# Layer 2 of a four-layer graph network: one block-diagonal projection in banks of its own, and the pair's preparation on other units

## The chip, the cores and the metric

The kernel runs on one core of a Trainium2 chip. The metric is the device time of one launch in microseconds, the median of several runs. The profile is of one further execution. Its abbreviations: PE is TensorE's matmul, PEld its weight load, DVE is VectorE, ACT ScalarE, POOL GpSimd, SP SyncE.

## What is computed

Four graph layers follow each other on x of shape 16 x 1024 x 64 with one 1024 x 1024 adjacency matrix; after each comes a residual and a layer normalization. The change is in layer 2 (and touches code that layer 0 shares):

```python
def _L2_gnn_ref(input, adj, W, a):
    h = jnp.matmul(input, W)
    s1 = jnp.einsum('bnf,f->bn', h, a1)
    s2 = jnp.einsum('bnf,f->bn', h, a2)
    e = s1[:, :, None] + s2[:, None, :]
    e = jnp.where(e > 0, e, ALPHA * e)
    masked = jnp.where(adj[None, :, :] > 0, e, NEG_INF)
    attention = jax.nn.softmax(masked, axis=-1)
    h_prime = jnp.matmul(attention, h)
    return jax.nn.elu(h_prime)
...
x = _layernorm(x + _L0_gnn_ref(x, L0_gnn_W, L0_gnn_a, adj), axis=-1)
x = _layernorm(x + _L1_gnn_ref(x, ...), axis=-1)
x = _layernorm(x + _L2_gnn_ref(x, adj, L2_gnn_W, L2_gnn_a), axis=-1)
x = _layernorm(x + _L3_gnn_ref(x, adj, ...), axis=-1)
```

## The kernel before

Layers 0 and 2 are made by one function, `gat_layer`. A batch b has 1024 nodes, which lie as C = 8 chunks of P = 128; D = 64 features; HALF = 512, CH = 4. The attention weight of node m for node n is rewritten as a product in which the softmax's row factor cancels, so that a unit k (128 of the nodes summed over) is one DVE instruction, `e` = max(G, q) times the transposed adjacency (L959, 128 x 1024), and one `product` on PE: two matmuls (L971) with 64 value columns as weights, one for each half of 512 nodes. Their outputs lie on partitions 0 to 63 and 64 to 127 of one accumulator bank `y`. In layer 2 (`zero_mean`) the 64th value column holds p alone, since a feature whose mean is zero follows from the other 63, and this row of `y` is the softmax's sum.

After eight units a batch goes through its tail: `evict` copies `y` to SBUF (ACT, L989); `project` multiplies it by the weights on PE; `divide` takes the sums out of PSUM, inverts them and scales (DVE, L1014, L1016, two of L1019), then exponentiates for the elu (`m`, ACT, L1026); `residual` is two DVE operations (L1031, L1032); `norm` eight `bn_stats` (L1040), and for the second batch of a pair a chain of small operations for the moments; `root`, `shift` and `store` finish it (ACT, DVE, ACT: eight activations `x`, L775).

`project` in layer 2 has twelve matmuls: four with the two columns of `ind`, which pick the sums (L1001), and eight of 64 columns with `w_out` (128 x 64, the weights twice), each from one half of the partitions (L1005). They go into two tiles `po` of the pool `ps_t` (two banks, shared with the transposes and scores below).

The preparation is made for a pair of batches (b even, b + 1): `prep_x` transposes x in two halves (`pxT`, PE L898, copied by ACT, L899); `prep_s` has eight matmuls of 4 columns for the node scores (`ps`, L904); `prep_top` copies these on DVE (L912), takes a maximum, and reduces it over the partitions on POOL (`gtop`, L916); `prep_p` (`down`, `up` on DVE, p and q on ACT); `prep_G` in two halves, each two matmuls (`pg`, L939) and an exponential of ACT (L940); `prep_v` scales the values on ACT for one batch (eight of L946 and a copy).

Layer 2 is recorded under a manual schedule: the order in which the Python code issues instructions is the order on PE, ACT, DVE and POOL. The main loop goes over t (the batch) and k (the unit). In each step it issues `unit` (DVE) for k, then the `product` of two units earlier (LAG = 2), then the tasks that the dictionary `slots` holds for (t, k). A task of batch b is placed with `at(b + t, k, task)`. The tail of a batch stands at (1, 1), (1, 3), (1, 4), (1, 6), (1, 7), (2, 0), (2, 2) and `store` at (3, 6) or (3, 2), that is while the next batches' units run. So "unit 3" below is a place k = 3 in the step of some batch t; in an even t the transposes, scores and top of the next pair are placed, in an odd t p and G. Layer 0 isn't under the manual schedule.

[...] In layer 2 the pools `ps_t` (2), `ps_a` (2, for `y`) and `ps_g` (2) take six. Layer 3 starts behind layer 2 with other pools; its `project` has the form that the change brings to layer 2, with `wb` as the weights (L1276, L1280, L1286).

Of the kernel before, what the change touches and what calls it, by code (L numbers as in the profile page):

```python
# [8 lines left out]
F32 = mybir.dt.float32  # L9
# [4 lines left out]
ALU = mybir.AluOpType  # L14
AX = mybir.AxisListType

P = 128
# [561 lines left out]
def fast_path(  # L579
# [24 lines left out]
    nc = tc.nc  # L604
    B, N, D = x.shape
    C = N // P
# [5 lines left out]
    HALF = N // 2  # L612
    CH = C // 2

    const = ctx.enter_context(tc.tile_pool(name="const", bufs=1))
# [71 lines left out]
    def bc_last(ap, n):  # L687

        return ap.unsqueeze(2).to_broadcast([P, ap.shape[1], n])
# [150 lines left out]
    def gat_setup(w, name, zero_mean):  # L840
        wd, w1, w4, ind, a_sb = (w[k] for k in ("wd", "w1", "w4", "ind", "a"))
        wT = const.tile([D, P], F32, tag=f"{name}_wT", name=f"{name}_wT")
        transposed(wT, wd, P, D)
        pa = ps_t.tile([P, HALF], F32, tag="t", name=f"{name}_pa")
        nc.tensor.matmul(pa[:, :2], wT, a_sb, start=True, stop=True)
        wa = const.tile([P, 2], F32, tag=f"{name}_wa", name=f"{name}_wa")
        nc.vector.tensor_copy(wa, pa[:, :2])
        nc.vector.tensor_scalar(w1, ones, wa[:, 0:1], None, ALU.mult)
        nc.vector.memset(w4, 0.0)
        nc.vector.memset(ind, 0.0)  # L850
        for i in range(2):
            rows = slice(i * D, (i + 1) * D)
            nc.vector.tensor_copy(w4[rows, i : i + 1], wa[rows, 0:1])
            nc.vector.tensor_copy(w4[rows, 2 + i : 3 + i], wa[rows, 1:2])
        if zero_mean:


            less = const.tile([P, P], F32, tag=f"{name}_less", name=f"{name}_less")
            nc.vector.tensor_copy(less, ident)
            for i in range(2):  # L860
                rows = slice(i * D, (i + 1) * D)
                end = (i + 1) * D - 1
                nc.vector.tensor_scalar(
                    less[rows, rows], ident[rows, rows], ident[rows, end : end + 1], None, ALU.subtract
                )
                nc.vector.tensor_copy(ind[rows, i : i + 1], ident[rows, end : end + 1])
            pw = ps_t.tile([P, HALF], F32, tag="t", name=f"{name}_pw")
            nc.tensor.matmul(pw[:, :D], less, wd, start=True, stop=True)
            w_out = const.tile([P, D], F32, tag=f"{name}_wo", name=f"{name}_wo")
            nc.vector.tensor_copy(w_out, pw[:, :D])  # L870
        else:
            w_out = wd

            for r in range(4):
                rows = slice(r * 32, (r + 1) * 32)
                nc.vector.tensor_copy(ind[rows, r % 2 : r % 2 + 1], ident[rows, r * 32 : r * 32 + 1])
        w["out"] = w_out

    def gat_layer(w, name, zero_mean, extra, first, own, ordered):
# [7 lines left out]
        xT, G, pq, vals, only, stats = {}, {}, {}, {}, {}, {}  # L887
# [10 lines left out]
                nc.tensor.transpose(pt[:, j, :], x_pair(b, h * CH + j), ident)  # L898
            nc.scalar.copy(xT[b][:, h * HALF : (h + 1) * HALF], pt.rearrange("p j q -> p (j q)"))  # L899

        def prep_s(b):
            pt = ps_t.tile([P, HALF], F32, tag="t", name="ps12")
            for c in range(C):
                nc.tensor.matmul(  # L904
                    pt[:, 4 * c : 4 * c + 4], xT[b][:, c * P : (c + 1) * P], w4, start=True, stop=True
                )
            pq[b] = pt

        def prep_top(b):
            pt = pq[b]  # L910
            s = s12[:, b // 2]
            nc.vector.tensor_copy(s, pt[:, : 4 * C].rearrange("p (c f) -> p c f", f=4))  # L912
            top = small.tile([P, 1], F32, tag="top", name="top")
            nc.vector.tensor_reduce(top, s[:, :, 2:4], AX.XY, ALU.max)
            gtop = small.tile([P, 1], F32, tag="gtop", name="gtop")
            nc.gpsimd.partition_all_reduce(gtop, top, P, bass_isa.ReduceOp.max)  # L916
            pq[b] = gtop

        def prep_p(b):
            gtop = pq[b]  # L920
            down = small.tile([P, 1], F32, tag="down", name="down")
            nc.vector.tensor_scalar(down, gtop, -1.0, None, ALU.mult)
            up = small.tile([P, 1], F32, tag="up", name="up")
            nc.vector.tensor_scalar(up, gtop, 1.0 - ALPHA, None, ALU.mult)
            s2 = s12[:, b // 2, :, 2:4]
            p = small.tile([P, C, 2], F32, tag="p", name="p")
            nc.scalar.activation(p, s2, AF.Exp, bias=down)
            q = small.tile([P, C, 2], F32, tag="q", name="q")
            nc.scalar.activation(q, s2, AF.Exp, bias=up, scale=ALPHA - 1.0)
            pq[b] = (p, q, up)  # L930
# [23 lines left out]
        def attention(b):  # L954
# [40 lines left out]

            def project():
                y, t = held["s"]
                pos = [ps_t.tile([P, HALF], F32, tag="t", name="po") for _ in range(2)]
                tot = pos[0][:, CH * D : CH * D + 2 * CH].rearrange("p (j h) -> p j h", h=2)
                for j in range(CH):  # L1000
                    nc.tensor.matmul(tot[:, j, :], t[:, j * P : (j + 1) * P], ind, start=True, stop=True)  # L1001
                for j in range(CH):
                    for h, po in enumerate(pos):
                        rows = slice(h * D, (h + 1) * D)
                        nc.tensor.matmul(  # L1005
                            po[:, j * D : (j + 1) * D], y[rows, j * P : (j + 1) * P], w_out[rows, :],
                            start=True, stop=True,
                        )
                held["p"] = pos, tot

            def divide():
                pos, tot = held["p"]
                total = sums[:, b, :]
                nc.vector.tensor_scalar(total.rearrange("p (h j) -> p j h", h=2), tot, 1e-30, None, ALU.max)  # L1014
                rt = small.tile([P, C], F32, tag="rt", name="rt")
                nc.vector.reciprocal(rt, total)  # L1016
                held["v"] = ep.tile([P, C, D], F32, tag="v", name="v")
                for h, po in enumerate(pos):
                    nc.vector.tensor_tensor(  # L1019
                        held["v"][:, h * CH : (h + 1) * CH, :],  # L1020
                        po[:, : CH * D].rearrange("p (j d) -> p j d", d=D),
                        bc_last(rt[:, h * CH : (h + 1) * CH], D), ALU.mult,
                    )

                held["m"] = ep.tile([P, C, D], F32, tag="m", name="m", bufs=4)
                nc.scalar.activation(held["m"], held["v"], AF.Exp)  # L1026

# [36 lines left out]
            slots.setdefault((t, k), []).append(task)  # L1064

        work = [attention(b) for b in range(B)]
        for b in range(B):
            end = (3, 6) if b % 2 == 0 else (3, 2)
            for task, (t, k) in zip(work[b][2], ((1, 1), (1, 3), (1, 4), (1, 6), (1, 7), (2, 0), (2, 2), end)):
                at(b + t, k, task)  # L1070
        ahead = []
        for b in range(0, B, 2):
            chain = [(lambda b=b, h=h: prep_x(b, h), -2, h) for h in range(2)]
            chain += [(lambda b=b: prep_s(b), -2, 2), (lambda b=b: prep_top(b), -2, 3)]
            chain += [(lambda b=b: prep_p(b), -1, 1)]
            chain += [(lambda b=b, h=h: prep_G(b, h), -1, 2 + h) for h in range(2)]
            chain += [(lambda b=b: prep_v(b), -1, 4), (lambda b=b: prep_v(b + 1), 0, 4)]
            for task, t, k in chain:
                if b + t < 0:
                    ahead.append(task)  # L1080
                else:
                    at(b + t, k, task)
# [127 lines left out]
    def prep_v(b):  # L1210
        v = l3a.tile([P, C, D], F32, tag="vals", name=f"vals_{b}")
        nc.scalar.copy(v[:, :, : D - 1], xb(b)[:, :, : D - 1])
        nc.vector.memset(v[:, :, D - 1 : D], 1.0)
        vals[b] = v
# [421 lines left out]
                at(b + t, p, task, where)  # L1636

    with tc.tile_pool(name="ps_g", bufs=1, space=bass.MemoryType.PSUM, reuse_waits="tile") as ps_g, tc.tile_pool(
        name="gat2", bufs=2, reuse_waits="tile"
    ) as gp:  # L1640
        places = [(15, j) for j in (0, 1, 2, 3, 4, 5, 6, 7)]
        extra = {p: [task] for p, task in zip(places, ahead)}
        for p, task in zip(((0, 0), (0, 1), (0, 3), (0, 7), (1, 3), (1, 7)), last):
            extra.setdefault(p, []).append(task)

        def first(ahead):
            for task in ahead:
                task()

        ending = gat_layer(later["w2"], "l2", True, extra, first, 5, True)  # L1650
# [128 lines left out]
```

## Time and profile before

| | us |
|---|---|
| median of 3 runs | 2162.24 (2161.66 to 2167.61) |
| the profiled execution | 2170.64 |
| its span, first to last instruction | 2168.8 |
| layer 0, first product to last projection | about 31 to 297 |
| layer 2, first `e` to the last projection's end | 467.7 to 728.3 |
| `e` of a unit, DVE, from one to the next | 1.20 |
| a product (two matmuls), PE, back to back at full and half clock | 0.86, 1.72 |
| `pxT`, four transposes | 0.65 |
| eight `bn_stats` | 1.03 |

The page counts time as busy when an instruction was on the engine; a matmul of fp32 shows as two records, so "x8" is four matmuls. In timeline lines the first number is the start, the second the time covered, and in square brackets stands the engine's idle time just before it with what ended it. The clock is the share of TensorE's full speed that was granted.

### The profile page before, as it was taken

The numbers are of one execution on the slowest core, as the hardware profiler recorded it, in microseconds if no ns is written. First come the engines' busy times: TensorE is split into PE (matmuls) and PEld (weight loads), VectorE is DVE, ScalarE is ACT, GpSimd is POOL, SyncE is SP. The second block draws the span as 40 slices with busy tenths as digits, with TensorE's granted clock in tenths as the row PEclk, the third lists the DMA queues.
The fourth block names the chain that finished last, engine by engine and source line by source line (L and its number), as shares of the span: only waits on it lengthen the run. The fifth ranks groups of instructions, "written<-read, shape, count | busy, mean of one in ns | idle before, by whom it ended". The sixth has DMA issues, their size and how long they took to land.

```text
span 2168.8 us, 26641 instructions
## 1 busy us (share of the span) xinstructions
PE 2047.2 (94%) x10321; PEld 866.2 (40%) x10321; DVE 1852.5 (85%) x3221; ACT 1227.5 (57%) x1965; POOL 51.0 (2%) x77
## 2 busy tenths in 40 slices
PE   7999979998898899999999999999999999999993
PEld 3333347753433333333333333333333433343331
DVE  5888889978988877798898898889889889888997
ACT  4454556555535666566655665655665665565541
POOL 0000000000000000000000000000000000000001
PEclk8999989988978999999999999999999999999997
DMA  6000000000000200000000000000000000000000
GB/s 162 1 1 1 1 1 1 1 1 1 1 1 1 72 6 1 1 1 6 1 6 5 1 6 1 6 5 1 6 6 1 6 1 6 6 1 6 1 7 15
DMA packets 23656, 18.92 MB, mean 9 GB/s; under 512 B 19361, under 2 KB 19426, under 8 KB 23522
## 3 DMA queue, kind: packets, MB, share of 16 engines
q1 hardware_dynamic: 23218, 17.11, 2.8%
q8 instruction: 83, 1.36, 0.3%
q14 instruction: 51, 0.42, 0.1%
q10 hardware_dynamic: 304, 0.03, 0.0%
HBM read 12.95 MB, written 4.19 MB: 8 GB/s over the span
## 4 chain that ended last, share of the span: by engine, by line
PE 73%; DVE 21%; ACT 4%; issue 1%; DMA 0%; POOL 0%; SPq 0%; POOLq 0%; DVEq 0%; ACTq 0%
PE y L1259 18%; PE s L1247 17%; PE y_l L971 8%; PE s L1344 5%; PE y L1371 4%; DVE e L1252 4%; PE u_l L982 3%; DVE e L959 3%; PE po L1276 3%; PE po L1531 3%; PE po L1005 2%; PE pg L939 2%; PE po L1001 1%; PE ps L904 1%; ACT e L1251 1%
## 5 line engine op out<-in xcount | busy, mean ns | idle before, releaser
L1251 ACT ACTIVATE e<-s,shift 128x1024 f32<-128x1024 f32 x512 | 542.9, 1111 | 243.2 <-PE s L1247 237.8
L1252 DVE TENSOR_TENSOR e<-e,aT 128x1024 f32<-128x1024 f32 x512 | 602.6, 1220 | 87.7 <-ACT e L1251 85.6
L1247 PE MATMUL s<-hT 64*128 64x512 f32 x2048 | 509.9, 612 | 15.5 <-DVE top L1188 8.6
L1259 PE MATMUL y<-e,vals 128*64 128x512 f32 x2048 | 490.6, 601 | 3.2 <-ACT yT L1266 1.3
L959 DVE SCALAR_TENSOR_TENSOR e<-G_l,q,aT 128x1024 f32<-128x1024 f32 x256 | 319.9, 1276 | 20.5 <-ACT G_l L940 12.4
L971 PE MATMUL y_l<-e,vals_l 128*64 128x512 f32 x1024 | 278.8, 660 | 27.9 <-DVE e L959 26.3
L1247 PEld LDWEIGHTS s<-hT 64*128 64x128 f32 x2048 | 182.5, 186 | 256.0 <-issue 170.8
L1259 PEld LDWEIGHTS y<-e,vals 128*64 128x64 f32 x2048 | 131.0, 136 | 330.6 <-issue 258.0
L1349 ACT ACTIVATE e<-s,shift 128x1024 f32<-128x1024 f32 x128 | 141.8, 1113 | 85.1 <-PE s L1344 74.9
L1351 DVE TENSOR_TENSOR me<-e,aT 128x1024 f32<-128x1024 f32 x128 | 155.8, 1220 | 16.8 <-ACT e L1349 16.5
L1362 DVE SCALAR_TENSOR_TENSOR junk<-e,aN 128x1024 bf16<-128x1024 f32 x128 | 155.9, 1218 | 0.2
L1371 PE MATMUL y<-me,h2v 128*64 128x512 f32 x512 | 135.3, 609 | 10.5 <-DVE me L1351 10.4
L1344 PE MATMUL s<-h2T 64*128 64x512 f32 x512 | 136.3, 610 | 4.6 <-DVE h2v L1331 4.4
L971 PEld LDWEIGHTS y_l<-e,vals_l 128*64 128x64 f32 x1024 | 65.3, 146 | 184.9 <-issue 75.4
L1531 PE MATMUL po<-hi,aR 128*128 128x512 f32 x256 | 101.9, 398 | 2.7 <-ACT hi L1516 1.1
L775 ACT ACTIVATE x<-m,bn_shift,bn_rstd 128x64 f32<-128x64 f32 x256 | 88.7, 432 | 23.2 <-DVE bn_shift L766 23.2
L1531 PE MATMUL po<-lo,aR 128*128 128x512 f32 x256 | 99.8, 391 | 0.0
L1306 ACT COPY zT<-pzT 128x1024 f32<-128x1024 f32 x32 | 32.4, 1012 | 78.3 <-PE pzT L1305 78.3
L1276 PEld LDWEIGHTS po<-wb,yT 128*128 128x128 f32 x512 | 62.0, 190 | 34.0 <-issue 21.1
L1276 PE MATMUL po<-wb,yT 128*128 128x130 f32 x512 | 73.8, 287 | 1.3 <-ACT e L1251 1.2
L982 PE MATMUL u_l<-e,only 128*32 128x512 f32 x512 | 72.0, 612 | 0.0
L1344 PEld LDWEIGHTS s<-h2T 64*128 64x128 f32 x512 | 46.6, 186 | 63.7 <-issue 41.4
(214 smaller groups left out, 2019.9 us busy)
## 6 DMA issues: line engine op xcount, KB each, us to landing
adj<-in_adj_dram SPq DMA_DIRECT2D x16, 512.0 KB, 4.4
x<-in_x_dram SPq DMA_DIRECT2D x16, 256.0 KB, 5.0
out_dram<-res SPq DMA_DIRECT2D x16, 256.0 KB, 2.0
wl<-in_L_gnn_Wh_dram SPq DMA_DIRECT2D x2, 64.0 KB, 5.3
wo<-in_L_gnn_Wo_dram SPq DMA_DIRECT2D x1, 64.0 KB, 5.0
l_wd<-in_L_gnn_W_dram ACTq DMA_DIRECT2D x2, 16.0 KB, 4.7
l_wd<-in_L_gnn_W_dram SPq DMA_DIRECT2D x2, 16.0 KB, 2.0
bo<-in_L_gnn_bo_dram SPq DMA_DIRECT2D x1, 32.0 KB, 3.3
```

The source lines that it names most:

```text
L959: nc.vector.scalar_tensor_tensor(e, G[b - b % 2][:, b % 2, :], pq[b - b % 2][1][:, k, b % 2 : b % 2 + 1], aT[:, k, :], ALU.max, ALU.mult,)
L971: nc.tensor.matmul(held["y"][h * D : (h + 1) * D, :], vals[b][:, k, :], e[:, h * HALF : (h + 1) * HALF], start=(k == 0), stop=(k == C - 1),)
L1247: nc.tensor.matmul(s[:, i, :], hT[rows, k * P : (k + 1) * P], hT[rows, cols], start=True, stop=True)
L1251: nc.scalar.activation(e, s, AF.Exp, bias=shifts[b, n])
L1252: nc.vector.tensor_tensor(e, e, bc_mid(aT[:, k, cols], 2), ALU.mult)
L1259: nc.tensor.matmul(held[h][i * D : (i + 1) * D, :], vals[b][:, k, :], e[:, i, :], start=(k == 0), stop=(k == C - 1),)
L1276: nc.tensor.matmul(o[:, j // 2, j % 2, :], held["y"][:, c * P : (c + 1) * P], wb[:, n, :], start=True, stop=True,)
L1344: nc.tensor.matmul(s[:, i, :], hT[rows, (i + k // CH) % 2, k % CH * P : (k % CH + 1) * P], hT[rows, 0, :], start=True, stop=True,)
L1351: nc.vector.tensor_tensor(m, e, aT[:, k, :].rearrange("p (i q) -> p i q", i=2), ALU.mult)
L1362: nc.vector.scalar_tensor_tensor(junk, held.pop(k).rearrange("p i q -> p (i q)"), 1.0, aN[:, k, :], ALU.mult, ALU.mult, accum_out=sums[:, ...
L1371: nc.tensor.matmul(held["o"][h * D : (h + 1) * D, :], vals["out", b][:, k, :], e[:, h, :], start=(k == 0), stop=(k == C - 1),)
L1531: nc.tensor.matmul(po.rearrange("p q k f -> p (q k f)"), aR[:, k, ic * P : (ic + 1) * P], e[:, k].rearrange("p q k f -> p (q k f)"), start ...
```

## The change

In `gat_setup`, for layer 2, `w_out` becomes 128 x 130: the weights as two diagonal blocks, zeros elsewhere, and the two columns of `ind` behind them. In `project` one matmul for each of four chunks then gives both halves and their sums; outputs go to a tile of two banks from a new pool `ps_p`, two chunks to a bank. `divide` reads this layout with four-dimensional views; layer 0 keeps its matmuls and gets the same views of its own layout. The preparation in layer 2 is placed anew, with `prep_s` cut in two halves of four chunks; layer 0 keeps its places.

```diff
-            w_out = const.tile([P, D], F32, tag=f"{name}_wo", name=f"{name}_wo")
-            nc.vector.tensor_copy(w_out, pw[:, :D])
+            w_out = const.tile([P, P + 2], F32, tag=f"{name}_wo", name=f"{name}_wo")
+            nc.vector.memset(w_out, 0.0)
+            for i in range(2):
+                rows = slice(i * D, (i + 1) * D)
+                nc.vector.tensor_copy(w_out[rows, i * D : (i + 1) * D], pw[rows, :D])
+            nc.vector.tensor_copy(w_out[:, P : P + 2], ind)
...
-        def prep_s(b):
-            pt = ps_t.tile([P, HALF], F32, tag="t", name="ps12")
-            for c in range(C):
+        def prep_s(b, chunks):
+            if chunks[0] == 0:
+                pq[b] = ps_t.tile([P, HALF], F32, tag="t", name="ps12")
+            for c in chunks:
                 nc.tensor.matmul(
...
             def project():
                 y, t = held["s"]
+                if zero_mean:
+                    pt = ps_p.tile([P, 2, HALF], F32, tag="p", name="po")
+                    o = pt[:, :, : 2 * (P + 2)].rearrange("p t (c f) -> p t c f", c=2)
+                    for j in range(CH):
+                        nc.tensor.matmul(
+                            o[:, j // 2, j % 2, :], y[:, j * P : (j + 1) * P], w_out, start=True, stop=True
+                        )
+                    held["p"] = [o[:, :, :, h * D : (h + 1) * D] for h in range(2)], o[:, :, :, P : P + 2]
+                    return
                 pos = [ps_t.tile([P, HALF], F32, tag="t", name="po") for _ in range(2)]
...
-                nc.vector.tensor_scalar(total.rearrange("p (h j) -> p j h", h=2), tot, 1e-30, None, ALU.max)
+                nc.vector.tensor_scalar(total.rearrange("p (h t c) -> p t c h", h=2, t=2), tot, 1e-30, None, ALU.max)
...
                     nc.vector.tensor_tensor(
-                        held["v"][:, h * CH : (h + 1) * CH, :],
-                        po[:, : CH * D].rearrange("p (j d) -> p j d", d=D),
-                        bc_last(rt[:, h * CH : (h + 1) * CH], D), ALU.mult,
+                        held["v"][:, h * CH : (h + 1) * CH, :].rearrange("p (t c) d -> p t c d", t=2), po,
+                        rt[:, h * CH : (h + 1) * CH].rearrange("p (t c) -> p t c", t=2).unsqueeze(3).to_broadcast(
+                            [P, 2, 2, D]
+                        ), ALU.mult,
                     )
...
             chain = [(lambda b=b, h=h: prep_x(b, h), -2, h) for h in range(2)]
-            chain += [(lambda b=b: prep_s(b), -2, 2), (lambda b=b: prep_top(b), -2, 3)]
-            chain += [(lambda b=b: prep_p(b), -1, 1)]
-            chain += [(lambda b=b, h=h: prep_G(b, h), -1, 2 + h) for h in range(2)]
-            chain += [(lambda b=b: prep_v(b), -1, 4), (lambda b=b: prep_v(b + 1), 0, 4)]
+            if zero_mean:
+                chain += [(lambda b=b, h=h: prep_s(b, range(h * CH, (h + 1) * CH)), -2, 5 + h) for h in range(2)]
+                places = (-2, 7), (-1, 1), (-1, 4), (-1, 6), (-1, 2)
+            else:
+                chain += [(lambda b=b: prep_s(b, range(C)), -2, 2)]
+                places = (-2, 3), (-1, 1), (-1, 2), (-1, 3), (-1, 4)
+            chain += [(task, *place) for task, place in zip((
+                lambda b=b: prep_top(b), lambda b=b: prep_p(b), lambda b=b: prep_G(b, 0),
+                lambda b=b: prep_G(b, 1), lambda b=b: prep_v(b),
+            ), places)]
+            chain += [(lambda b=b: prep_v(b + 1), 0, 4)]
...
     with tc.tile_pool(name="ps_g", bufs=1, space=bass.MemoryType.PSUM, reuse_waits="tile") as ps_g, tc.tile_pool(
+        name="ps_p", bufs=1, space=bass.MemoryType.PSUM, reuse_waits="tile"
+    ) as ps_p, tc.tile_pool(
         name="gat2", bufs=2, reuse_waits="tile"
     ) as gp:
```

More of the change, by code (lines that the diff above doesn't have):

```diff
@@ L899, in prep_x @@
             nc.scalar.copy(xT[b][:, h * HALF : (h + 1) * HALF], pt.rearrange("p j q -> p (j q)"))
-        def prep_s(b):
-            pt = ps_t.tile([P, HALF], F32, tag="t", name="ps12")
-            for c in range(C):
+        def prep_s(b, chunks):
+            if chunks[0] == 0:
+                pq[b] = ps_t.tile([P, HALF], F32, tag="t", name="ps12")
+            for c in chunks:
                 nc.tensor.matmul(
-                    pt[:, 4 * c : 4 * c + 4], xT[b][:, c * P : (c + 1) * P], w4, start=True, stop=True
+                    pq[b][:, 4 * c : 4 * c + 4], xT[b][:, c * P : (c + 1) * P], w4, start=True, stop=True
                 )
-            pq[b] = pt
         def prep_top(b):
@@ L1008, in project @@
                         )
-                held["p"] = pos, tot
+                held["p"] = (
+                    [po[:, : CH * D].rearrange("p (t c d) -> p t c d", t=2, d=D) for po in pos],
+                    tot.rearrange("p (t c) h -> p t c h", t=2),
+                )
             def divide():
@@ L1066, in gat_layer @@
         work = [attention(b) for b in range(B)]
+        ends = ((1, 1), (1, 3), (1, 4), (1, 6), (1, 7), (2, 0), (2, 2))
         for b in range(B):
             end = (3, 6) if b % 2 == 0 else (3, 2)
-            for task, (t, k) in zip(work[b][2], ((1, 1), (1, 3), (1, 4), (1, 6), (1, 7), (2, 0), (2, 2), end)):
+            for task, (t, k) in zip(work[b][2], (*ends, end)):
                 at(b + t, k, task)
```

## The prediction

> **What bounds the kernel now.** I read the page first, then busy times by stage, then who waited for whom on VectorE inside layer 2, then the timeline there. On the page:
>
> ```profile
> PE 2047.2 (94%) x10321; PEld 866.2 (40%) x10321; DVE 1852.5 (85%) x3221; ACT 1227.5 (57%) x1965; POOL 51.0 (2%) x77
> ...
> PE   7999979998898899999999999999999999999993
> ...
> PEclk8999989988978999999999999999999999999997
> ```
>
> PE (TensorE) looks like the bound everywhere, but PEclk dips in slices 9 to 13, which is layer 2 (about 467 to 728 us). The busy times of four stretches (layers 0, 1, 2, 3) show that layer 2 is different:
>
> ```profile
> 60.00:300.00 240.00, 236.64 (x1520) 87.27 (x1516) 202.18 (x450) 117.43 (x321) 3.06 (x6) 1.00 0.00 1
> 320.00:456.00 136.00, 132.54 (x646) 108.48 (x645) 130.82 (x297) 81.11 (x159) 0.00 (x0) 1.00 0.00 1
> 467.00:728.00 261.00, 230.56 (x1144) 101.77 (x1144) 220.60 (x464) 128.45 (x376) 9.34 (x9) 0.83 0.02 7
> 740.00:2100.00 1360.00, 1336.80 (x6501) 515.13 (x6500) 1180.22 (x1762) 826.55 (x978) 27.26 (x45) 1.00 0.02 5
> ```
>
> Columns: stretch, length, then busy us of PE, PEld, DVE, ACT, POOL, then the granted clock. Layers 0 and 3 keep PE 98% busy at clock 1.00. In layer 2 PE has 30 us of idle and a clock of 0.83, and DVE (VectorE) has 40 us of idle. For what DVE waited, in the list of waits between 470 and 735 us (total, times, longest):
>
> ```profile
> DVE l_sums L1014 <- PE po L1005: 29.5, 12, 4.0
> DVE v L1031 <- ACT m L1026: 2.5, 2, 1.7
> ...
> DVE l_s L912 <- PE ps L904: 1.7, 2, 1.2
> ```
>
> One wait dominates: `divide` on DVE waits for the last matmul of `project`. The timeline of one even batch shows why PE is late there:
>
> ```profile
> 563.64 1.95 PE L904 MATMUL ps<-l_w,xT_l 128*128 128x4 f32 x16
> ...
> 566.53 1.05 PE L1001 MATMUL po<-l_ind,yT_l 128*128 128x2 f32 x8
> ...
> 567.51 1.83 PE L1005 MATMUL po<-l_wo,yT_l 64*128 64x64 f32 x16
> ...
> 569.37 0.17 DVE L1014 TENSOR_SCALAR l_sums<-po 128x8 f32<-128x8 f32 x1 [1.80 <-PE po L1005]
> ```
>
> Within 5.6 us PE runs eight small matmuls for the scores (`prep_s`), one attention product, then twelve small ones for the projection. DVE stands 1.80 us. The counter-example is batch 14, which has no pair left to prepare:
>
> ```profile
> 696.63 1.05 PE L1001 MATMUL po<-l_ind,yT_l 128*128 128x2 f32 x8
> ...
> 697.61 1.11 PE L1005 MATMUL po<-l_wo,yT_l 64*128 64x64 f32 x16
> ...
> 699.07 0.17 DVE L1014 TENSOR_SCALAR l_sums<-po 128x8 f32<-128x8 f32 x1
> ```
>
> No idle stands in brackets: the same long projection without the preparation ahead of it is hidden behind DVE's units.
>
> DVE's floor: from `divide` at 487.88 to the one six pairs later at 686.05 are 198.2 us, 33.0 a pair, of which the idle entries of the timeline sum to 27.4 (25.3 at L1014, 1.7 at L1031, 0.4 at L912). So 28.5 us a pair is DVE's own work.
>
> [...] stretches of 2 us in layer 2 stand at 0.50 or 1.00 or on an edge between (566 to 568: 0.93, 568 to 570: 0.50), and the dips follow either idle (608 to 612, PE busy 1.76 of 4 us) or the run of small matmuls above. [...] (at 492.47 `m` came only after eight `x` of L775 queued ahead, and DVE stood 1.66 us for it). [...] The pools then hold 2+2+2+2 banks. [...]
>
> **The change part by part.**
>
> *Projection.* Twelve matmuls a batch go, four of 128x130 come. The old ones take 2.02 us on PE at full clock (696.63 to the next product at 698.65), 3.7 at half (631.43 to 635.14). Layer 3 has the new form already (L1276):
>
> ```profile
> 758.55 1.16 PE L1276 MATMUL po<-wb,yT 128*128 128x130 f32 x8
> 759.64 2.85 PE L1247 MATMUL s<-hT 64*128 64x512 f32 x12
> ```
>
> So 1.09 us, 0.93 less; at half clock it isn't shown, between 1.09 (if issue sets it) and 2.18; I take 1.9. The DVE part keeps its sizes: L1280 and L1286 of layer 3 read the same layout at 171 and 419 ns, L1014 and L1019 take 170 and 419, so 0. The bank pair of its own removes waits for `ps_t` buffers (at most what batch 15 shows, PE held before 711.42 by `hsq`); I take 0 to 0.5 us once, and 0 in the sum. In exchange layer 3's third score tile has to wait for batch 15's `divide` if it lies on these banks: v ends some 1.3 us after the projection, two tiles ahead of it take 1.7, so 0.
>
> *`prep_s` and `prep_top`.* The 1.88 us of eight score matmuls leave the place ahead of `project` (unit 2) for units 5 and 6, in two halves. Their new neighbours are the units where `divide` (1.12), `residual` (1.30) and `norm` (1.03, with moments 1.9) keep DVE away from making `e`, so PE has room there. `prep_top` moves past `norm` to unit 7; its POOL reduction (1.24) now has two units of 1.20 until `down` instead of six. Cover 2.4 against about 1.5, cost 0.
>
> *`prep_G`.* Two matmuls (0.95 each half, 2.0 cold) leave units 2 and 3 for 4 and 6, so the odd batches lose the first half ahead of `project`. What is queued on ACT matters: in the changed order it is `m`, G half 0, eight `x` of a stored batch, G half 1, and DVE's first unit of the next batch needs half 1. From the end of `v`: `m` 0.67, G 1.11, eight `x` 2.76, G 1.11, sum 5.7. DVE from there: two units 2.4, residual 1.3, a unit 1.2, `bn` 1.03, sum 5.9. It just fits; I charge 0.15 us a pair, 1 in all, and up to 1.4 a pair if PE is cold there.
>
> *`prep_v`* of an even batch goes to unit 2 (2.1 us of ACT), before `m` is wanted 2.4 us and more later: 0. No DMA moves, and SP's and POOL's order is unchanged.
>
> *Set-up*: a memset and three small copies on DVE in layer 0 (0.4 us), which PE bounds: 0.
>
> What remains of the wait: at full clock, from `e1`'s end PE needs a product (0.86 to 1.08) and 1.09, DVE three units (3.6): slack 1.4 us. Entirely at half clock, even batch, from `e7`'s end: products 3 x 1.72, transposes 1.1, projection 1.9, sum 8.2, against `bn` 1.03 and five units 6.0: 1.2 us late. In an odd batch DVE has moments 0.9, top 0.35 and shift 0.7 besides and PE no transposes, so nothing is late. Dips will not go away (at the end of even batches PE still waits for DVE), so I leave 0.4 us for each of seven even batches, 3 us.
>
> Sum on the profile: removed 27.4 (L1014 without the last batch), 1.7 (L912), 0.9 (the last projection, where PE sets the pace into layer 3), 30.0; left 3 and 1. Gain 26, so 2170.6 (span 2168.8 and 1.9 around it) becomes 2144.6. What is late next is DVE itself. The median of the runs is 2162.2, 8.4 below the profiled run. Either profiling added that everywhere (then 2136), or the profiled run had more dips in layer 2, the only long stage without a clock of 1.00 (then its extra wait is part of the 26, and 2144.6 stands). I can't tell which and take the middle, 2140.
>
> **The rivals.**
> (1) *PE goes on being late.* Spreading the small matmuls leaves PE with less work and as many gaps, and dips fall on every even batch: 7 x 1.2 of projection and 7 x 1.0 of late G, 15 of 30 remain. Time 2162.2 - 12 = 2150. For it: dips at 512, 612, 646 and 677 begin where DVE starves PE, and that stays. Against: PE recovers within 3 to 7 us, before unit 3 in most.
> (2) *Slower: the clock falls.* PE's work a pair at full clock is then 16 products x 0.86, 1.3, 1.9, 1.9 and 2 x 1.09, about 21 us. Against 28.5 of DVE it is busy 74% only; if the clock stays low for it, a pair takes 21/clock, and that passes the present 33.0 plus 0.9 (6.5 us over seven pairs) below a clock of 0.62. At 0.58 it is 36 us a pair, +22, 2184. Against: a cold PE is a full PE, and full stretches restored it every time here; no stretch of 40 us in layer 2 is below 0.76.
> (3) *The G chain.* If half 1 comes 1.5 us late in each pair, 10 us are given back: 2150.
> (4) *The waits were hidden anyway*: would need layer 3 to absorb them. It has PE 98% busy, so an earlier start is an earlier end: 2162.
>
> **How the numbers follow.** Forecast 0.72, (1) 0.14, (3) 0.07, (4) 0.03, (2) 0.04. The floor for the range: all 30 removed and the profile's 8.4 off, 2132. The top: rivals (1) and (3) with the unprofiled base uncertain, 2152. A difference of 0.3% (6.5 us) is what can be told from no change. Faster: the forecast, (1) and (3), 0.93; within 0.3%: (4), 0.03; slower: (2), 0.04.
>
> **What would show it.** Right: L1014's successor waits less than 5 us in all in layer 2, the pair period is 28.5 to 29.5, DVE over 95% busy between 480 and 700 us, the four wide matmuls take about 1.1 us, layer 3 keeps its length. Wrong: a clock below 0.75 in layer 2, DVE's `e` waiting for G by over 1 us a pair, `down` waiting for POOL, or `m` late for `residual`.

## The result, and the profile after

| | us | ratio to before, 95% interval |
|---|---|---|
| before, median of 4 | 2161.95 (2159.52 to 2167.61) | |
| after, median of 4 | 2132.02 (2130.08 to 2138.12) | 0.9861 [0.9838, 0.9883] |
| after, the unaltered kernel once more, median of 4 | 2132.49 (2130.50 to 2133.27) | 0.9857 [0.9840, 0.9874] |

The change takes 30 us off as timed. 2140 was forecast, with a range from 2132 to 2152: a gain of 22 us. The measured gain is 8 us larger and lies on the edge of the range. The profiled execution fell from 2170.64 to 2138.12 us, by 32.5.

The page of the changed kernel, engines, slices, granted clock and the shares of the chain that ended last:

```profile
PE 2017.2 (94%) x10065; PEld 841.9 (39%) x10065; DVE 1851.9 (87%) x3224; ACT 1227.7 (57%) x1965; POOL 51.2 (2%) x77
...
PE   7999979999887999999999999999999999999993
...
PEclk9999989989999999999999999999999999999997
...
PE 69%; DVE 25%; ACT 3%; issue 1%; DMA 0%; POOL 0%; SPq 0%; POOLq 0%; DVEq 0%; ACTq 0%
```

Read alone, this page hides what happened: PE is still the busiest engine, at the same 94%. The slices that differ much are those of layer 2 (9 to 13): PEclk has no 7 there any more, and PE still has dips to 8 and 7. The busy times by stretch, first of before for the middle of layer 2 (stretch, length, then PE, PEld, DVE, ACT, POOL busy, clock):

```profile
480.00:690.00 210.00, 188.00 (x934) 83.27 (x932) 177.89 (x372) 98.39 (x289) 7.41 (x6) 0.84 0.00 1
```

and of after:

```profile
60.00:300.00 240.00, 235.59 (x1514) 87.00 (x1512) 201.99 (x449) 117.64 (x321) 3.06 (x6) 1.00 0.00 1
320.00:456.00 136.00, 132.52 (x646) 108.55 (x645) 130.47 (x294) 80.82 (x159) 0.00 (x0) 1.00 0.00 1
480.00:690.00 210.00, 183.88 (x840) 68.83 (x840) 206.45 (x441) 118.00 (x341) 9.00 (x8) 0.94 0.01 4
740.00:2090.00 1350.00, 1324.23 (x6442) 512.00 (x6440) 1167.55 (x1736) 812.26 (x952) 27.25 (x45) 1.00 0.01 3
```

In 210 us of layer 2 DVE is now busy for 206.45 (98%), where it was 177.89 (85%). The other layers read as before. What DVE still waits for between 465 and 715 us, in the list of waits of after (total, times, longest):

```profile
DVE e L964 <- ACT G_l L945: 5.9, 1, 5.9
DVE l_sums L1032 <- PE po L1007: 3.1, 2, 2.8
DVE e L1278 <- ACT e L1277: 1.8, 1, 1.8
DVE shift L1221 <- POOL gtop L1216: 0.8, 2, 0.4
DVE l_s L917 <- PE ps L910: 0.5, 1, 0.5
```

The 29.5 us at `divide` have become 3.1, and 2.8 of these are the very last projection. The 5.9 are the start of the layer, ahead of its first `e` (before had 5.5 there); L1278 belongs to layer 3. The timeline of an even batch, to be held against the one at 563 us of before, with the scores (L910) now behind the projection:

```profile
553.34 1.16 PE L1007 MATMUL po<-l_wo,yT_l 128*128 128x130 f32 x8
...
555.78 0.17 DVE L1032 TENSOR_SCALAR l_sums<-po 128x8 f32<-128x8 f32 x1
...
556.30 1.05 PE L910 MATMUL ps<-l_w,xT_l 128*128 128x4 f32 x8
```

The projection ends 1.3 us ahead of `divide`, which has no idle in brackets. Before, it ended as DVE stood.

Counting layer 2 from its first `e` to the last `divide` in both profiles, and adding DVE's idle entries in the timeline between:

| | before | after |
|---|---|---|
| layer 2 | 260.6 (467.69 to 728.30) | 226.6 (469.05 to 695.66) |
| of it DVE waits | 37.0 | 4.4 |
| of it DVE's own work | 223.6 | 222.2 |
| layer 3, from there to the end of the span | 1440.5 | 1440.6 |

Layer 2 became 34.0 us shorter, 32.6 of them waits. It began 1.4 us later and layer 3 kept its length within 0.1: that is the 32.5.

### The profile page after: what moved, and what is told of

Same layout as the page of the kernel before. It is cut to its first block, busy times and chain, and to the rows that moved or that the text cites. A ratio compares the mean times of both kernels' runs of the same rounds, so it can differ in the third digit from the quotient of the medians.

```text
span 2136.3 us, 26123 instructions
## 1 busy us (share of the span) xinstructions
PE 2017.2 (94%) x10065; PEld 841.9 (39%) x10065; DVE 1851.9 (87%) x3224; ACT 1227.7 (57%) x1965; POOL 51.2 (2%) x77
## 4 chain that ended last, share of the span: by engine, by line
PE 69%; DVE 25%; ACT 3%; issue 1%; DMA 0%; POOL 0%; SPq 0%; POOLq 0%; DVEq 0%; ACTq 0%
PE y L1285 18%; PE s L1273 17%; DVE e L964 7%; PE y_l L976 6%; PE s L1370 5%; PE y L1397 4%; DVE e L1278 4%; PE u_l L987 3%; PE po L1302 3%; PE po L1557 3%; ACT e L1277 1%; PE pg L944 1%; DVE r L1566 1%; PE pzT L1331 1%; PE ps L910 1%
## 5 line engine op out<-in xcount | busy, mean ns | idle before, releaser
L1278 DVE TENSOR_TENSOR e<-e,aT 128x1024 f32<-128x1024 f32 x512 | 602.7, 1221 | 87.3 <-ACT e L1277 85.3
L976 PE MATMUL y_l<-e,vals_l 128*64 128x512 f32 x1024 | 271.3, 637 | 26.5 <-DVE e L964 25.8
L976 PEld LDWEIGHTS y_l<-e,vals_l 128*64 128x64 f32 x1024 | 60.7, 139 | 169.8 <-issue 57.1
```

The costliest lines, as they stand in the source:

```text
L976: nc.tensor.matmul(held["y"][h * D : (h + 1) * D, :], vals[b][:, k, :], e[:, h * HALF : (h + 1) * HALF], start=(k == 0), stop=(k == C - 1),)
L1278: nc.vector.tensor_tensor(e, e, bc_mid(aT[:, k, cols], 2), ALU.mult)
```

## The experiments

The theory was that of the prediction: DVE is the floor of layer 2, PE was late at `divide`, and both a shorter projection and the removal of work ahead of it take that lateness away. The rivals were that one of the two parts does it alone, that the clock and not the order sets it, or that the banks do it.

Below, "layer 2" and "DVE waits" are counted as in the table above. The times of several kernels on one chip share their runs of before; ratios are to be compared, not microseconds across groups.

| kernel | median us | ratio, interval | layer 2 | DVE waits | clock 480:690 |
|---|---|---|---|---|---|
| before | 2161.95 | | 260.6 | 37.0 | 0.84 |
| after, repeated | 2132.49 | 0.9857 [0.9840, 0.9874] | 225.2 | 3.0 | 0.93 |
| wide projection alone | 2150.87 | 0.9943 [0.9924, 0.9962] | 245.6 | 22.1 | 0.87 |
| new places alone | 2146.32 | 0.9924 [0.9903, 0.9945] | 234.8 | 11.8 | 0.92 |
| places of G and v back | 2141.73 | 0.9901 [0.9879, 0.9923] | 231.4 | 8.5 | 0.93 |
| places of the scores back | 2143.46 | 0.9915 [0.9897, 0.9933] | 233.3 | 10.2 | 0.91 |
| before, PE kept busy | 2163.05 | 0.9994 [0.9983, 1.0005] | 253.7 | 29.6 | 0.95 |
| old projection, own banks, new places | 2144.78 | 0.9910 [0.9894, 0.9927] | 230.2 | 7.8 | 0.93 |
| after, scaling on ACT | 2131.04 | 0.9840 [0.9823, 0.9858] | 217.9 | 5.8 | 0.97 |
| the same, G earlier | 2131.01 | 0.9847 [0.9824, 0.9869] | 218.3 | 6.2 | 0.95 |

**One part alone: the wide projection with the old places.** The branch of the new places is not taken:

```diff
             chain = [(lambda b=b, h=h: prep_x(b, h), -2, h) for h in range(2)]
-            if zero_mean:
+            if False:
                 chain += [(lambda b=b, h=h: prep_s(b, range(h * CH, (h + 1) * CH)), -2, 5 + h) for h in range(2)]
```

> Only the wide projection in banks of its own; the preparation keeps its old places. Theory (DVE's pace is the floor of layer 2 and only what shortens PE's way to divide counts): each of the eleven waits of before at divide loses 0.93 us where the clock was full and about 1.9 where it was half, some 15 us of 27; 2147, and 12 us of waiting at l_sums left in layer 2. Rival A (the shorter projection is the whole gain): 2134 or less. Rival B (the places are the whole gain): 2158 or more.

Measured 0.9943 [0.9924, 0.9962]. The list of waits of DVE over layer 2 keeps the old wait at about half its size:

```profile
DVE l_sums L1032 <- PE po L1007: 16.2, 15, 2.3
...
DVE l_s L917 <- PE ps L910: 3.2, 2, 2.1
DVE v L1049 <- ACT m L1044: 1.8, 1, 1.8
```

From 29.5 to 16.2 at `divide` is 13.3, which isn't spread evenly. By the timeline, the six batches whose projection stands behind the scores waited 18.0 us before and wait 6.1 now; the seven behind the halves of G waited 9.4 and still wait 8.6. The shorter projection takes length out of the waits, mostly behind the scores, but leaves a wait in 15 of 16 batches, where before had one in 12. 2147 was expected, and 12 us of waits.

**The other part alone: new places with the old projection** (the 128 x 64 weight and the twelve matmuls, in `ps_t`):

```diff
-            w_out = const.tile([P, P + 2], F32, tag=f"{name}_wo", name=f"{name}_wo")
...
+            w_out = const.tile([P, D], F32, tag=f"{name}_wo", name=f"{name}_wo")
+            nc.vector.tensor_copy(w_out, pw[:, :D])
...
-                if zero_mean:
+                if False:
                     pt = ps_p.tile([P, 2, HALF], F32, tag="p", name="po")
```

> Only the new places; the projection stays at twelve matmuls in the shared pool. Theory: even batches lose 1.9 to 2.3 us of score matmuls ahead of the projection, odd ones 1.0 to 2.0 of G, what is left is the cold even batches, some 6 us; 2140. Rival A: 2155 or more. Rival B: within 3 us of the changed kernel, 2133. If parts overlap as the theory says, the gains of this run and of the wide projection alone add up to more than the 30 us of both.

Measured 0.9924 [0.9903, 0.9945], and in its list of waits of DVE:

```profile
DVE l_sums L1028 <- PE po L1015: 6.2, 6, 2.1
DVE e L960 <- ACT G_l L941: 3.0, 2, 1.6
```

A batch that met a cold PE, in the timeline of the same kernel:

```profile
650.41 1.87 PE L1011 MATMUL po<-l_ind,yT_l 128*128 128x2 f32 x8
652.21 1.98 PE L1015 MATMUL po<-l_wo,yT_l 64*128 64x64 f32 x16
654.11 1.97 PE L972 MATMUL y_l<-e,vals_l 128*64 128x512 f32 x4
```

From 650.41 to 654.11 are 3.70 us of the old projection at half clock (0.50 there); `divide` stood 0.98 us for it, and the late PE then made `G` late for an `e` by 1.40 (at 662.93). The new one takes 2.01 at nearly half clock (in the chain below). Ahead of the hand-over to layer 3 four waits at `divide` are left, 2.8 us: 1.02 and 0.98 on a cold PE, 0.65 at full clock, and 0.15. So in this profile the places take away most of the waits, and the short projection has the rest to take, most of it in cold batches. 2140 was expected.

Both parts are needed. As timed they add up: 0.57% and 0.76% against 1.39% to 1.43% together, within the intervals. By the profiles they overlap: layer 2 falls by 15.0 and 25.8, together more than the 34.0 of both. So the kernel with the new places alone was profiled a second time.

> The new places alone, for a second profile: its timed median (2146.3) lies 4.5 us above its first profile, which had 13 us of DVE waits in layer 2. Theory (the first profile was a lucky one; with the long projection the waits come and go with the dips): 15 to 22 us of waits here. Rival (something outside layer 2): 13 us again at a longer time.

It ran 2141.35 us with layer 2 at 234.4 us and waits of 11.3, where 15 to 22 had been expected: the sum repeated, though the waits fell on other batches (1.35 at 565.78; the first profile had its longest of this kind, 1.02, at 537.41). But the runs without a profile took 2140.5 to 2149.3, four of five above both profiled ones. The waits of a run without a profile can't be seen, so whether the parts overlap stays open.

**Half of the placement undone: G and v on their old places.**

```diff
-                places = (-2, 7), (-1, 1), (-1, 4), (-1, 6), (-1, 2)
+                places = (-2, 7), (-1, 1), (-1, 2), (-1, 3), (-1, 4)
```

> The changed kernel with both halves of G and the values of the even batch back at units 2, 3 and 4. Theory: the odd batches' waits of before (2.05, 2.32, 1.32, 1.33, 2.36) come back less 0.93 each, 4 to 5 us; 2137. A rival that G's new place matters for ACT only: 2132, no wait at l_sums.

**The other half: the scores in one piece on their old place.**

```diff
-                chain += [(lambda b=b, h=h: prep_s(b, range(h * CH, (h + 1) * CH)), -2, 5 + h) for h in range(2)]
-                places = (-2, 7), (-1, 1), (-1, 4), (-1, 6), (-1, 2)
+                chain += [(lambda b=b: prep_s(b, range(C)), -2, 2)]
+                places = (-2, 3), (-1, 1), (-1, 4), (-1, 6), (-1, 2)
```

> The changed kernel with the eight score matmuls whole at unit 2 and the top at unit 3 again. Theory: the even batches' waits of before (1.44, 3.66, 1.80, 4.01, 3.81, 3.28) come back less 0.93 to 1.9 each, some 8 us; 2140. A rival that the small matmuls matter by the clock: the mean clock of layer 2 falls from 0.92 to about 0.83 and the loss is over 12 us; 2145.

**And the changed kernel unaltered**, to know how far two measurements of one kernel lie apart.

> The changed kernel unaltered, timed beside the experiments. The two single parts measured alone gave 0.57% and 0.76% of the time, their sum 1.33%, close to the 1.39% of both: as timed they add up, where the theory (parts overlap above DVE's floor) wants a sum larger than the whole, as the profiles have it (layer 2 shorter by 15.0 and 25.8 us, by 34 with both). If they add up, the changed kernel stays near 2134 here; if they overlap and the earlier comparison was off, it is 2138 or more.

By the ratios G and v back cost 0.44% (0.9901 to 0.9857), 9.5 us; the scores back cost 0.58%, 12.5 us. 4 to 5 and some 8 had been expected, and in the profiles layer 2 is 6.2 and 8.1 us longer than in the repeated kernel; the rest lies outside it or in the runs that have no profile. The waits over layer 2 rise from 3.0 to 8.5 and to 10.2, mostly at `divide` (5.3 and 7.5). So each half of the placement is worth something.

The mean clock hardly differs with the scores back (0.91 against 0.93), and yet it matters in single batches. Here are two batches of that kernel, the scores and then the projection of each:

```profile
519.02 1.95 PE L910 MATMUL ps<-l_w,xT_l 128*128 128x4 f32 x16
...
522.78 1.92 PE L1007 MATMUL po<-l_wo,yT_l 128*128 128x130 f32 x8
...
548.97 1.95 PE L910 MATMUL ps<-l_w,xT_l 128*128 128x4 f32 x16
...
551.86 1.16 PE L1007 MATMUL po<-l_wo,yT_l 128*128 128x130 f32 x8
```

In the first the clock was 0.50 from 521 to 524 us, right behind the scores, and `divide` waited 1.69 us; in the second it stayed at 1.00 and `divide` did not wait. All waits over 1 us at `divide` in these two kernels, the very last projection apart, have a stretch at half clock ahead of them: 1.69, 1.64 and 1.67 with the scores back, 1.58 and 1.38 with G back. The others are 0.2 to 0.5. What stands ahead of the projection costs most where PE is cold, and the mean of the stage hides that. With G and v back the 1.8 us of `residual` waiting for `m` return too: on ACT the second half of G (487.10) and eight `x` of a stored batch (488.11) run ahead of `m` (490.76).

**Is it the clock? Before, with PE kept busy.** In the kernel before, bf16 matmuls (128 x 512, result unused) are added in batches 1 to 14, four at unit 0 and four or eight at unit 1, so that PE doesn't idle there:

```diff
+        if zero_mean:
+            idle = ps_w.tile([P, HALF], F32, tag="w", name="warm")
+
+            def warm(n):
+                for _ in range(n):
+                    nc.tensor.matmul(idle, ident16, aT[:, 0, :HALF], start=True, stop=True)
+
+            for t in range(1, B - 1):
+                at(t, 0, lambda: warm(4))
+                at(t, 1, lambda n=4 + t % 2 * 4: warm(n))
```

> The kernel before, with idle matmuls (bf16, 128x512, results unused) put on PE behind the products of units 0 and 1 of batches 1 to 14, where PE stands waiting for DVE. They add no dependency. Theory (half of the waits at divide comes from the clock that falls in those idle places): the clock of layer 2 goes from 0.83 to 0.95 or more, the waits that remain are those at full clock, 1.4 us in each even batch, and the time falls by 10 to 17 us, to about 2150. Rival (the order of the work on PE is all, the clock follows from it): within 4 us of before, or slower since PE has more to do.

The ratio is 0.9994 [0.9983, 1.0005]: nothing, where 10 to 17 us had been expected. Yet the clock did rise; its busy times in layer 2 and its list of waits there:

```profile
480.00:690.00 210.00, 203.74 (x1087) 88.33 (x1097) 186.29 (x387) 106.12 (x308) 7.41 (x6) 0.95 0.00 1
```

```profile
DVE l_sums L1014 <- PE po L1005: 21.9, 12, 5.1
```

0.95 is more than the changed kernel has, and DVE still stands 21.9 us at the same line. In the timeline `divide` waits exactly 1.44 us at 540.22, 601.86 and 663.51; ahead of the second the old projection takes its 2.02 us of full clock (599.74 to 601.76, clock 1.00 there), so this wait is not one of cold matmuls. Layer 2 is 6.9 us shorter in this profile than in that of before; the runs don't show it. By the timeline of before PE's gaps in layer 2 are 2.5 us at most, at a mean clock of 0.84 from 480 to 690 us; with the added matmuls they are 1.7 at most behind the layer's start, and the clock rose to 0.95 without a gain in time. The added matmuls occupy PE themselves: in the first batch they stand ahead of the projection, and its wait grew from 2.05 to 5.06. In the other batches the waits at `divide` fell from 27.5 to 16.9 in this profile. So it isn't shown that a free warm-up would bring nothing, and the clock probably has a share in the waits; it is shown that a clock of 0.95 with this order leaves more than half of them.

**Is it the banks? The old projection with the new places, in the tile of two banks.** It is the kernel with new places alone, with one edit more:

```diff
-                pos = [ps_t.tile([P, HALF], F32, tag="t", name="po") for _ in range(2)]
+                if zero_mean:
+                    pt = ps_p.tile([P, 2, HALF], F32, tag="p", name="po")
+                    pos = [pt[:, i, :] for i in range(2)]
+                else:
+                    pos = [ps_t.tile([P, HALF], F32, tag="t", name="po") for _ in range(2)]
```

> The new places and the old twelve matmuls, but their tiles in the two banks of their own. Theory (the shared pool delays nothing, the banks are worth 0 beside the shorter projection): the same as the places alone, 2146 +- 3. Rival (waiting for a buffer of the shared pool was part of the lateness): 2140 or less, half way to the changed kernel.

0.9910 [0.9894, 0.9927] against 0.9924 [0.9903, 0.9945] without the banks: the intervals overlap, so the banks are worth nothing that can be told. What lies between 0.9910 and 0.9857 is the shorter projection itself.

**The bound now: take DVE work away.** If DVE is the floor, less work on it must shorten a pair one for one. The two multiplications of L1037 (0.76 us a batch, 1.5 a pair) become eight activations on ACT in layer 2, and `residual` and the even `store` move by one unit each to make room:

```diff
+                for c in range(C if zero_mean else 0):
+                    h, j = c // CH, c % CH
+                    nc.scalar.activation(
+                        held["v"][:, c, :], pos[h][:, j // 2, j % 2, :], AF.Copy, scale=rt[:, c : c + 1]
+                    )
-                for h, po in enumerate(pos):
+                for h, po in enumerate([] if zero_mean else pos):
...
-        ends = ((1, 1), (1, 3), (1, 4), (1, 6), (1, 7), (2, 0), (2, 2))
+        ends = ((1, 1), (1, 3), (1, 4), (1, 7 if zero_mean else 6), (1, 7), (2, 0), (2, 2))
...
-            end = (3, 6) if b % 2 == 0 else (3, 2)
+            end = (3, 7 if zero_mean else 6) if b % 2 == 0 else (3, 2)
```

> The changed kernel with the scaling in divide moved from DVE (two of 0.38 us a batch) to ACT (eight of 0.25), the residual one unit later and the store of the even batch behind the second half of G. Theory (DVE's own work is layer 2's only bound now): 16 x 0.75 = 12 us less, 2122 if the changed kernel takes 2134. Rival (PE, or ACT at 75% busy, is next at once): within 4 us of the changed kernel, with new waits of DVE for m or G of 0.7 us or more a batch.

Pairs without a wait take 26.75 us where the changed kernel takes 28.17: 1.42 for 1.5 moved. So DVE is the bound of layer 2. 12 us had been expected, and the time gained little: 0.9840 [0.9823, 0.9858] against 0.9857 [0.9840, 0.9874], which overlap. Layer 2 in the profile is 7.3 us shorter than in the repeated kernel's, but it began 5.3 us later (468.89 to 463.56) and layer 3 took 1443.1 against 1439.9. The later start lies ahead of everything edited in layer 2, and the two profiles of before (at the end of this section) differ by nearly as much. The longer layer 3 is in part an effect: the last batch is scaled on ACT too (687.88 to 689.59), PE waits 2.04 us for that ahead of score products of layer 3, and DVE's first `e` there comes 3.7 us late instead of 1.6. In part it may not be: layer 3 also took 1442.0 to 1442.8 in three kernels that scale on DVE (the new places alone, the scores back, the old projection in its own banks). And ACT has become a second bound; in the list of waits of DVE:

```profile
DVE e L964 <- ACT G_l L945: 8.3, 4, 5.9
DVE e L1283 <- ACT e L1282: 3.7, 1, 3.7
```

Three of the four waits for G (0.8 each) are in the pairs; the fourth is the layer's start. L1283 is the first of layer 3.

**The same with G one unit earlier**, to free these three:

```diff
-                places = (-2, 7), (-1, 1), (-1, 4), (-1, 6), (-1, 2)
+                places = (-2, 7), (-1, 1), (-1, 3), (-1, 5), (-1, 2)
```

> The scaling on ACT as before, with the halves of G at units 3 and 5 instead of 4 and 6, since DVE waited 0.8 us for G in three batches there. Theory (DVE is the bound): these waits go, every pair takes 26.8 us, layer 2 some 10 us less than in the changed kernel; 2122 to 2126. Rival (G ahead of the scaling on ACT makes m late, or pg on PE holds products): no better than 2131.

The three waits went, four pairs in the middle take 26.74 to 26.96, and in their place came one at `residual` and one at the hand-over to layer 3:

```profile
DVE e L1283 <- ACT e L1282: 4.2, 2, 3.7
DVE v L1054 <- ACT m L1049: 2.3, 1, 2.3
DVE top L1219 <- PE pn L1215: 2.1, 1, 2.1
```

0.9847 [0.9824, 0.9869]; neither version can be told from the changed kernel, where 2122 to 2126 us had been expected.

**The kernel before once more, a second profiled execution**, to see whether its layer 2 repeats.

> The kernel before, for a second profile. The first took 2170.6 us and had 37 us of DVE waits in layer 2 (all of them, from the first e to the last l_sums); the timed runs are 2162. If the first profile only had more dips of the clock, this one has fewer waits, about 30, and layer 2 takes 6 to 8 us less; if profiling adds time everywhere, the waits are 35 or more again.

It ran 2166.41 us, with layer 2 again 260.6 us long and every wait in it equal within 0.02 us. What differs is the start of layer 2: 463.10 here, 467.69 in the first. Of these 4.6 us 3.5 are there already at the last projection of layer 0 (291.81 and 295.35).

## Why the prediction was right in kind and too small

The mechanism held: PE was late at `divide`, its lateness went, and DVE's own work is what remains. What failed is the sum, 22 us of gain from the median against 30 measured: three terms were mis-sized, and the base was set too high.

Right, with its numbers: DVE's floor was given as 28.5 us a pair and 28.17 is measured. The wide projection takes 1.09 us from start to the next product (553.34 to 554.43). At half clock it takes 2.03 (the last one, 693.53 to 695.56, clock 0.50), near the 1.9 taken and within its bounds. L1032 and L1037 keep their 170 and 420 ns. G half 1 "just fits": its exponential ends at 549.29 and DVE's first `e` with it starts at 549.81. The POOL reduction is covered (POOL done at 537.45, `down` at 538.35 without a wait). No transfer became late, layer 3 kept its length, and the rival of a falling clock did not appear: the clock rose from 0.84 to 0.94. (The hold before 711.42 that it names was one of the weight load; PE itself had no idle there. It had put 0 on it.)

The dips stayed, as the prediction said, and cost next to nothing. The chain of waits of the changed kernel shows the one that came nearest, where the clock between 592 and 600 us was 0.50 to 0.69:

```profile
590.06 1.03 DVE bn L1058 x8
...
593.73 3.68 PE y_l L976 x8
597.41 2.01 PE po L1007 x8
599.42 0.02 issue
599.44 0.18 DVE l_sums L1032
```

Two products (eight records) and a projection, almost all at half clock, make `divide` wait 0.24 us, the only such wait ahead of the last batch. Of the cold stretches at 510, 538, 566, 593, 616 and 650 us (clock 0.50 to 0.62 over 2 us) five follow 2.5 us of idle PE at the end of a batch. The one at 616 does not: PE had no gap of 0.2 us since 593.7, and the clock fell, to 0.58 from 616 to 618, right behind the second half of the scores. The batches whose projection comes right behind one of the five are those in which DVE has the moments and the scores' maximum to do besides (590.06 to 592.39 in the chain), and where PE has no transposes. In the others the clock is back at 1.00 by then (at the projections of 525.17, 553.34, 581.51, 610.25 and 638.20 us).

By the terms of its sum, on the profile:

| term | forecast | measured | in the second profile |
|---|---|---|---|
| wait at `divide`, without the last batch | 27.4 - 3 | 27.4 - 0.24 | 27.4 - 0.9 |
| `l_s` waiting for the scores | 1.7 | 1.65 - 0.52 | 1.65 |
| the last projection | 0.9 | -0.7 (2.14 to 2.81) | 0.9 (2.14 to 1.22) |
| `residual` waiting for `m` | not counted | 2.5 | 2.5 |
| first maximum of layer 3 (`top` for `pn`) | not counted | 2.3 | 2.3 |
| late G | -1 | 0 | 0 |
| `shift` | not counted | 0.1 | 0.1 |
| DVE's own work | 0 | 1.4 | 1.4 |
| sum, with its rounding | 26 | 34.0 | 35.4 |

The three terms: "I leave 0.4 us for each of seven even batches, 3 us" put the cost of the dips on the batches where they do not fall; 0.24 was left in the first profile, and 0.9 ahead of the last batch in the second (at 537.00, 621.87 and 678.80 us). "I charge 0.15 us a pair" for G: it cost nothing. And the 30.0 removed counted waits at three places only, while the list of waits quoted in the prediction showed the 2.5 at L1031, and the view also held 2.3 at L1188; in these too another engine serves DVE late, and they went as well. The last projection gave the 0.9 forecast in the second profile. In the first it ran wholly at half clock (0.50 from 692 to 696), and its wait grew. That DVE's own work came out 1.4 shorter is unexplained.

The base was the other half of the miss. "I can't tell which and take the middle" added 4 us: 26 off the median is 2136, 26 off the middle is 2140. The second profile of before tells part of it. Its layer 2 repeats, and it took 4.2 of the 8.4 us between the first profiled run and the median less: the layer began 4.6 us earlier, layer 3 took 0.4 longer. Ahead of layer 2 all these kernels have nearly the same work, and their profiles begin it at 462.3 to 463.6 or at 465.6 to 469.1 us. The rest stays open: with about equal starts (463.10 and 463.56) the two profiled executions differ by 35.9 us, where the medians differ by 30. Runs of before without a profile may thus have shorter waits than its profiles show. That the median came to lie on the floor of the range, 2132, is in part chance: the floor took the 30 us of counted waits and the whole 8.4 of the base off the profiled 2170.6, while the profiled executions lost 32.5 and 35.9.

Of the rivals, (1) and (3) are answered by the list of waits: 0.24 instead of 15 us at `divide` before the last batch, and no `e` waiting for G behind the layer's start. (4) falls with layer 3's unchanged length, and (2) with the clock.

## What to carry to other kernels

An engine that is 94% busy over the span may be too late in one stage and idle in the same stage: list what the other engine waits for there, and count every wait in the list that has the same cause, not only the largest. When a result is late, move what is queued ahead of it to places where the consumer is busy elsewhere, and shorten the result's own work; here each alone brought about half of the gain (0.57% and 0.76% of 1.39% to 1.43%). Look at the clock batch by batch, since the mean of a stage hides which waits stand behind a cold stretch. Once the waits are gone the consumer's work is the time, and moving a part of it pays one for one in the stage (1.42 us for 1.5 here, in a pair without a wait) only as long as the engine that takes it has room, which is seen in the next wait.

## What the runs showed of the hardware

Waits can repeat to 0.02 us from one profiled execution to the next, as all of layer 2 did in the two of before, although they differ by 4.2 us in total. They need not: in the second execution of the changed kernel and of that with the new places alone they fell on other batches (0.24 us at 599.44, then 0.28 to 0.34 at 537.00, 621.87 and 678.80; a longest of 1.02 at 537.41, then 1.35 at 565.78). At half clock a projection takes a little less than twice its time: the old one 2.02 and 3.70 us, the wide one 1.09 and 2.03, factors of 1.83 and 1.86. And the clock fell behind PE's idle stretches of 2.5 us (in the changed kernel to between 0.50 and 0.62, behind five of them), but also right behind the small score matmuls: in the changed kernel at 616 us, to 0.58, where PE had no gap of 0.2 us for 22 us, and with the scores back at 521 us, to 0.50. Why it fell there isn't shown.
